# First LayerNorm's inverse deviations by way of DRAM instead of the TensorE, with seven interleaved blocks

## The chip, the core and the metric

The kernel runs on one core of a Trainium2 chip. The metric is the device time in microseconds (us) of the whole launch; lower is better. Before the change three runs took 2405.96 us in the median (2402.36 to 2407.58). Engine names in the profile: PE is the TensorE's matmul side and PEld its weight loads, DVE is the VectorE, ACT the ScalarE, POOL the GpSimd, SP the SyncE, which only issues DMAs here.

## What is computed

Layer 0 adds to `x` (32 images, 56 x 56 places, 128 channels, f32) a convolution of its binarised group norm. Layer 1 reads the result as 32 x 3136 tokens of 128 channels and adds causal attention in windows of 64 tokens, and then an expert layer fed by 8 tokens for each of 64 experts. Cut to what matters:

```python
x = x + _L0_conv_ref(_gn(x), L0_conv_gamma, L0_conv_beta, L0_conv_W)
t = _to_tokens(x)
t = t + _L1_attn_ref(_ln_t(t), L1_attn_w_qkv, L1_attn_w_proj, L1_attn_b_proj)
t = t + _L1_ffn_ref(_ln_t(t), L1_ffn_gate_w, L1_ffn_gate_b, L1_ffn_weight1, L1_ffn_weight2)

def _ln_t(v, eps=1e-5):
    m = jnp.mean(v, axis=-1, keepdims=True)
    s = jnp.var(v, axis=-1, keepdims=True)
    return (v - m) / jnp.sqrt(s + eps)
```

The change concerns the first `_ln_t`, the one ahead of the attention. The mean's part is folded into centred weights ahead of the loop, so the kernel only multiplies each token by its inverse deviation.

## The kernel before

**Preparation** (lines 164 to 330). All of `x` is read once, in 16 loads of 3136 KB, for the statistics of the group norm; small products turn them into the thresholds `thr_a` and `thr_b`. SP's queue holds these 16 loads, then the loads of the main loop.

**Main loop** (lines 933 to 1022). The 32 images form 16 pairs; a block is 8 rows of a pair, so a pair has 7 blocks and there are 112. A block holds 2 x 448 tokens, as 7 units of 128 (64 tokens of each image). One turn of the loop works on several blocks at once: while block n is in its attention, later blocks are in earlier stages. With `n` the turn:

- `load` (line 463): block n+6 comes in, 2 DMAs of 224 KB on SP, into `xb` (two buffers).
- `bits` (475): block n+5 is turned to channels first (7 transposes `xT_ps`), copied by ACT (`xT`, `bn`) and binarised by DVE (`hbits`).
- `conv` and `residual` (502, 516): 9 products of block n+3, and `yT = xT + conv` on DVE. `conv` is split, 4 taps after `scores` and 5 after `norm1`.
- `norm1` (531): block n+2 is turned back (`yt`), DVE takes `bn_stats` of its 7 units, and POOL raises the variances to -0.5 (`inverse_std`, line 426). The result `rstd1` has a token on each partition: 128 x 7.
- `normalise` (534): block n+1. The next products want channels on partitions, so every channel's row needs all 896 inverse deviations. Seven transposes of a broadcast column write them to the PSUM tile `rr`, and DVE multiplies `rr` by `yT` into `n1T`.
- `queries_or_keys`, `values` (543, 561): products of `n1T`, each copied out by ACT.
- `scores` (598): block n; 4 mask products and 56 x 2 small products into two PSUM tiles, and two ACT exponentials `pT`.
- `attend` (631): the products `av` of `pT` and the values, then DVE's `rs` and `ao`; `turn_out`, `project`, `norm2` (658 to 695): `aoT`, `pj`, DVE's `tT`, the turn `tt`, ACT's copy `tok`, second LayerNorm statistics, and stores of `tok` on POOL's queue (to the output) and on SP's (to `toks`).
- `gate_logits` (697): block n-1, the products `lg`.

The order on PE, DVE, ACT, SP and POOL is the order of the program text (`manual_schedule`), so an instruction that waits holds up all behind it on its engine. PSUM tiles made by `bank2` rotate through three buffers. In one turn PE's order is `sc`, 4 taps `cv`, `rr`, `lg`, `av`, `xT_ps`, `qT_ps`, `aoT_ps`, `kT_ps`, `v_ps`, `pj`, `yt`, 5 taps `cv`, `tt`.

**A pair's end.** Over the 13 turns after a pair's last block its steps run in between (lines 898 to 924): `spread` sends the second LayerNorm's deviations to DRAM and back as rows (`devs`, `drow`), then come the largest 8 gate values, the gather of their tokens (`gather`, POOL), shares, and stores. In turns 1 to 8 the loop also fills the DRAM tensor `share` with zeros, 1024 KB a turn.

**Expert stage** (lines 1029 to 1193). After the loop the pooled tokens go through the experts and the results are added at their places in the output.

Of the kernel before, what the change touches and what calls it, by code (L numbers as in the profile page):

```python
# [17 lines left out]
P = 128  # L18
HEADS = 4
HD = 32  # L20
# [10 lines left out]
def kernel(  # L31
# [39 lines left out]


    ident = const.tile([P, P], F32, name="ident")
    make_identity(nc, ident)
# [7 lines left out]

    head1 = const.tile([P, HEADS, HD], F32, name="head1")
    nc.vector.memset(head1, 1.0)
# [10 lines left out]

    g4 = const.tile([P, P // 4, 4], F32, name="g4")
    nc.vector.memset(g4, 0.25)
# [10 lines left out]

    tri = const.tile([P, 2, P], F32, name="tri")
    nc.vector.memset(tri, 0.0)  # L110
# [53 lines left out]
    with tc.tile_pool(name="prep", bufs=1) as prep, tc.tile_pool(  # L164
# [118 lines left out]
        def scaled(b0, b1):  # L283
# [3 lines left out]
            nc.vector.tensor_mul(vr[:, bs], vr[:, bs], rg[:, bs])  # L287


        TP = 2 * S // P  # L290
        x2 = x.rearrange("b h w c -> (b h w) c").rearrange("(n p j) c -> n p j c", p=P, j=TP)
        for pr in range(NPAIR):
            xb = xs.tile([P, TP, C], F32, name="xb")
            nc.sync.dma_start(out=xb, in_=x2[pr])
            st = xs.tile([P, 2, NB, 6], F32, name="st")
            for g in range(NB):
                pt = xps.tile([P, 2, 512], F32, name="pt").rearrange("p a (s c) -> p (a s) c", c=P)
                for j in range(NU):
                    nc.tensor.transpose(pt[:, j, :], xb[:, g * NU + j, :], ident)
                for i in range(2):  # L300
                    nc.vector.bn_stats(st[:, i, g, :], pt[:, :NU, i * WIN : (i + 1) * WIN])  # L301
            for i in range(2):
                nc.vector.bn_aggr(
                    mv[:, 2 * pr + i, :], st[:, i].rearrange("p g s -> p (g s)")
                )
            if pr == NPAIR - 4:
                group_norm(0, B - 8)
            if pr == NPAIR - 2:
                scaled(0, B - 8)
        group_norm(B - 8, B)  # L310
        scaled(B - 8, B)
# [18 lines left out]
        nc.vector.tensor_scalar(thr_b, thr_b, off, None, ALU.add)  # L330


    slots = [dram.tile([P, K], F32, name=f"slots{i}") for i in range(NPAIR)]
    putrow = [dram.tile([P, K], U32, name=f"putrow{i}") for i in range(NPAIR)]
    grows = dram.tile([NQ, P, NPAIR, P], F32, name="grows")

    share = dram.tile([NQ, P, NPAIR, 2, ES], F32, name="share")
    toks = [dram.tile([2, S, P], F32, name=f"toks{i}") for i in range(NPAIR)]
    eout = dram.tile([E, B, P], F32, name="eout")
    obias_d = dram.tile([P, NG, P], F32, name="obias_d")  # L340
    devs = [dram.tile([2, NB * NU, WIN], F32, name=f"devs{i}") for i in range(NPAIR)]

# [24 lines left out]
    def main_loop(fast):  # L367
        with ExitStack() as main:
# [17 lines left out]
            )  # L386
            yTp = loop.enter_context(tc.tile_pool(name="yTp", bufs=4))
            w1 = loop.enter_context(tc.tile_pool(name="w1", bufs=1))
# [8 lines left out]
            def units(t):  # L397

                return t.rearrange("p a (s c) -> p (a s) c", c=P)[:, :NU, :]
# [9 lines left out]
            nc.gpsimd.memset(vblk, 1.0)  # L409
            zero = first.tile([P, 4 * P], F32, name="zero")  # L410
            nc.gpsimd.memset(zero, 0.0)

# [45 lines left out]
            class Block:  # L458
# [16 lines left out]
                def bits(self):  # L475

                    pr, r = self.pr, self.r
                    xT_ps = turn(self.xb, "xT_ps")
                    self.xT = xTp.tile([P, 2, BT], F32, name="xT")
                    nc.scalar.activation(  # L480
                        self.xT.rearrange("c i (p j) -> c i p j", j=NU),
                        units(xT_ps).rearrange("c j (i p) -> c i p j", p=WIN),
                        AF.Identity, bias=conv_nb,
                    )
                    bn = w1.tile([P, 2, RB, W], F32, name="bn")
                    for i in range(2):
                        b = 2 * pr + i
                        nc.scalar.activation(  # L488
                            bn[:, i].rearrange("c h (g j) -> c h g j", j=NU),
                            units(xT_ps)[:, :, i * WIN : (i + 1) * WIN].rearrange(  # L490
                                "c j (h g) -> c h g j", h=RB
                            ),
                            AF.Identity, bias=thr_b[:, b : b + 1], scale=thr_a[:, b : b + 1],
                        )
                    bit = w1.tile([P, RB, W], FP16, name="bit")
                    nc.vector.tensor_scalar(bit, bn[:, 0], 0.0, 1.0 / FINE, ALU.is_ge, ALU.mult)
                    nc.vector.scalar_tensor_tensor(
                        hbits[pr % 2][:, 1 + r * RB : 1 + (r + 1) * RB, 1 : 1 + W],
                        bn[:, 1], 0.0, bit, ALU.is_ge, ALU.subtract,
                    )  # L500
# [30 lines left out]
                def norm1(self):  # L531
                    self.rstd1 = unit_stats(units(turn(self.yT, "yt")), "ln1")

                def normalise(self):
                    rr = bank2("rr")
                    for u in range(NU):
                        nc.tensor.transpose(  # L537
                            units(rr)[:, u, :], self.rstd1[:, u : u + 1].to_broadcast([P, P]), ident
                        )
                    self.n1T = w1.tile([P, NU, P], F32, name="n1T")  # L540
                    nc.vector.tensor_mul(self.n1T, units(rr), self.yT)

# [164 lines left out]
            class Pair:  # L707
# [9 lines left out]
                def spread(self, r0, r1):  # L717
# [3 lines left out]
                    nc.tensor.transpose(dT_ps, self.devs[:, r0 * NU : r1 * NU], ident)  # L721
                    dT = wp.tile([m, P], F32, name=f"dT{m}")
                    nc.scalar.copy(dT, dT_ps)
# [143 lines left out]
                def shares(self, ks):  # L867

                    if ks[0] == 0:
                        self.sh = gatep.tile([P, E, K], F32, name="sh")  # L870
                    src = self.srow
# [60 lines left out]

            for n in range(-6, N + 1):
                this, nxt, conv, prev = at(n), at(n + 1), at(n + 3), at(n - 1)

                steps = [(n - pr * NB - NB + 1, pair) for pr, pair in pairs.items()]
                steps = [(j, pair) for j, pair in steps if 1 <= j <= 13]
                ends = dict(steps)
                if at(n + 6):
                    at(n + 6).load()  # L940
                if 0 < n <= NQ:
                    nc.sync.dma_start(
                        out=share[n - 1].rearrange("p n i s -> p (n i s)").rearrange(
                            "p (a s) -> p a s", s=4 * P
                        ),
                        in_=zero.unsqueeze(1).to_broadcast([P, NPAIR * 2 * ES // (4 * P), 4 * P]),
                    )
                if n == N // 8:
# [35 lines left out]
                if this:  # L984
                    this.attend()
                if at(n + 5):
                    at(n + 5).bits()
                if this and this.r == NB - 1 and n < N - 1:
# [23 lines left out]
                if this:  # L1012
                    this.project()
                if at(n + 2):
                    at(n + 2).norm1()
                if conv:
# [224 lines left out]
```

## Time and profile before

| what | value |
|---|---|
| median of three runs | 2405.96 us (2402.36 to 2407.58) |
| the profiled execution's own time | 2399.98 us |
| its span in the profile | 2398.2 us |
| PE / DVE / ACT / POOL busy in the span | 90% / 74% / 48% / 34% |
| mean granted TensorE clock | 0.959 |
| DMA share in the loop, by slices | 0.3 to 0.6 |
| preparation, up to the first `xT_ps` of the loop | 0 to 166 us |
| first to last `av` (112 blocks) | 201.5 to 2123 us |
| expert stage | from about 2145 us to the end |

In a group's row of the profile stand the line, engine, operation, output<-inputs, shapes and count, then the busy time and the mean of one instruction in ns, and the idle time before them with what ended it. In a row of the timeline the first number is the start and the second the duration, in us. A turn of the loop lasts 17.1 to 17.4 us for nearly all blocks, counted from one `av` to the next.

### The profile page before, as it was taken

How to read it: one execution, taken by the hardware profiler on the slowest of the kernel's cores; microseconds unless marked ns; L12 is line 12 of the kernel's file. 1: busy time of each engine (PE TensorE's matmuls, PEld its weight loads, DVE VectorE, ACT ScalarE, POOL GpSimd, SP SyncE). 2: the span in 40 equal slices, each digit the busy share in tenths (PEclk: the TensorE clock that was granted, in tenths of full speed). 3: DMA queues.
4: the chain of work that ended last, by engine and by line, in shares of the span. 5: the costliest groups of instructions: out<-in, count | busy, mean ns of one | idle time of the engine just before them, and what ended most of it. 6: DMA issues, size and time to landing. Idle time of an engine off the chain costs nothing.

```text
span 2398.2 us, 82838 instructions
## 1 busy us (share of the span) xinstructions
PE 2164.7 (90%) x35865; PEld 1524.2 (64%) x35865; DVE 1777.1 (74%) x4974; ACT 1159.6 (48%) x1683; POOL 814.3 (34%) x772
## 2 busy tenths in 40 slices
PE   6769999999999999999999999999999999954452
PEld 5656676667676666667676666666666767632332
DVE  7975567788888888888887878787878787775221
ACT  0015555555555556565655565656555555432210
POOL 1012223242424242424242333333333333334556
PEclk9989999999999999999999999999999999977776
DMA  9943464544444445454545363636363535647961
GB/s 367 393 153 84 138 166 101 119 112 107 109 111 105 115 102 118 99 120 97 122 98 122 82 137 80 139 80 139 79 137 81 135 84 127 189 124 259 356 231 58
DMA packets 238300, 334.31 MB, mean 139 GB/s; under 512 B 50598, under 2 KB 175206, under 8 KB 231654
## 3 DMA queue, kind: packets, MB, share of 16 engines
q1 hardware_dynamic: 207878, 254.56, 38.1%
q0 software_dynamic: 27648, 72.38, 13.0%
q8 instruction: 285, 4.67, 0.8%
q10 hardware_dynamic: 2400, 1.97, 0.3%
q14 instruction: 89, 0.73, 0.1%
HBM read 195.14 MB, written 134.74 MB: 138 GB/s over the span
## 4 chain that ended last, share of the span: by engine, by line
PE 77%; ACT 7%; DVE 6%; DMA 5%; issue 3%; POOL 2%; SPq 0%; POOLq 0%; ACTq 0%; DVEq 0%
PE cv L509 8%; PE av L639 8%; PE kT_ps L550 8%; PE pj L673 8%; PE v_ps L566 7%; PE sc L590 6%; PE xT_ps L440 4%; PE lg L701 4%; PE yt L440 4%; ACT bn L488 4%; PE rr L537 4%; PE tt L440 3%; ACT xT L480 3%; DVE st L301 3%; PE sc L579 2%
## 5 line engine op out<-in xcount | busy, mean ns | idle before, releaser
L426 POOL TENSOR_TENSOR ln_rstd<-ln_var,nhalf 128x7 f32<-128x7 f32 x112 | 167.6, 1496 | 924.9 <-DVE ln_var L423 609.4
L480 ACT ACTIVATE xT<-xT_ps,conv_nb 128x896 f32<-128x896 f32 x112 | 112.8, 1007 | 406.4 <-PE xT_ps L440 250.2
L426 POOL TENSOR_TENSOR devs<-ln_var,nhalf 128x7 f32<-128x7 f32 x112 | 165.7, 1479 | 266.4 <-DVE ln_var L423 266.4
L605 ACT ACTIVATE pT<-sc 128x896 f32<-128x896 f32 x224 | 193.2, 915 | 119.9 <-PE sc L590 118.9
L639 PEld LDWEIGHTS av<-vblk,pT 64*64 64x64 f32 x12544 | 195.7, 135 | 86.3 <-ACT pT L605 77.1
L509 PE MATMUL cv<-hbits,wconv 128*128 128x448 f16 x1008 | 233.0, 358 | 11.9 <-DVE s L524 5.6
L566 PEld LDWEIGHTS v_ps<-wqkvT,n1T 128*128 128x128 f32 x1568 | 192.7, 192 | 41.6 <-issue 41.6
L639 PE MATMUL av<-vblk,pT 64*64 64x33 f32 x12544 | 209.7, 221 | 6.2 <-issue 5.2
L679 DVE SCALAR_TENSOR_TENSOR tT<-pj,bproj_c,yT 128x448 f32<-128x448 f32 x224 | 142.7, 678 | 85.0 <-PE pj L673 85.0
L550 PE MATMUL kT_ps<-n1T,wqkvT 128*128 128x448 f32 x448 | 197.6, 563 | 5.5 <-PE aoT_ps L662 1.0
L673 PE MATMUL pj<-aoT,wprojT 64*128 64x448 f32 x896 | 200.2, 566 | 1.1 <-ACT aoT L665 1.1
L522 ACT ACTIVATE s<-cv,conv_mid 128x448 int32<-128x448 f32 x112 | 70.8, 632 | 257.1 <-PE cv L509 257.1
L566 PE MATMUL v_ps<-wqkvT,n1T 128*128 128x128 f32 x1568 | 193.1, 275 | 0.0
L550 PE MATMUL qT_ps<-n1T,wqkvT 128*128 128x448 f32 x448 | 188.1, 542 | 0.1
L692 POOL DMA_DIRECT2D out_dram<-tok x224 | 169.1, 756 | 0.1
L590 PE MATMUL sc<-qT,kT 32*64 32x64 f32 x12544 | 166.9, 233 | 0.0
L433 DVE BATCH_NORM_STATS2 ln_st<-yt 128x6 f32<-128x128 f32 x784 | 164.9, 280 | 2.5 <-PE yt L440 2.5
L590 PEld LDWEIGHTS sc<-qT,kT 32*64 32x64 f32 x12544 | 151.4, 130 | 22.7 <-issue 22.7
L433 DVE BATCH_NORM_STATS2 ln_st<-tok 128x6 f32<-128x128 f32 x784 | 161.8, 278 | 5.0 <-ACT tok L687 4.9
L1129 POOL DMA_INDIRECT out_dram<-f_rows,rowidx x128 | 123.8, 967 | 81.6 <-DVE f_rows L1125 44.7
L488 ACT ACTIVATE bn<-xT_ps,thr_b,thr_a 128x448 f32<-128x448 f32 x224 | 149.3, 720 | 2.6 <-DVE thr_b L330 2.4
L526 DVE SCALAR_TENSOR_TENSOR yT<-s,conv_s,xT 128x448 f32<-128x448 f32 x224 | 143.5, 682 | 4.0
(187 smaller groups left out, 4082.9 us busy)
## 6 DMA issues: line engine op xcount, KB each, us to landing
xb<-in_x_dram SPq DMA_DIRECT2D x16, 3136.0 KB
xb<-in_x_dram SPq DMA_DIRECT2D x224, 224.0 KB
toks<-tok SPq DMA_DIRECT2D x224, 224.0 KB
out_dram<-tok POOLq DMA_DIRECT2D x224, 224.0 KB, 3.5
u<-in_L_ffn_weight_dram SPq DMA_DIRECT2D x16, 2048.0 KB
drow<-devs SPq DMA_DIRECT2D x30, 672.0 KB
share<-zero SPq DMA_DIRECT2D x8, 1024.0 KB
grows<-rows SPq DMA_DIRECT2D x32, 256.0 KB
```

Of the source, the lines that this page charges most:

```text
L426: nc.gpsimd.tensor_tensor(rstd, var, nhalf[:, :n], ALU.pow)
L433: nc.vector.bn_stats(st[:, u, :], src[:, u, :])
L440: nc.tensor.transpose(units(t)[:, u, :], src[:, u, :], ident)
L480: nc.scalar.activation(self.xT.rearrange("c i (p j) -> c i p j", j=NU), units(xT_ps).rearrange("c j (i p) -> c i p j", p=WIN), AF.Identity ...
L488: nc.scalar.activation(bn[:, i].rearrange("c h (g j) -> c h g j", j=NU), units(xT_ps)[:, :, i * WIN : (i + 1) * WIN].rearrange("c j (h g) ...
L509: nc.tensor.matmul(self.cv[:, :BT], lhsT=wconv[:, t, :], rhs=hb[:, r * RB + kh : r * RB + kh + RB, kw : kw + W], start=(t == 0), stop=(t = ...
L550: nc.tensor.matmul(pp[:, a, :BT], lhsT=wqkvT[:, s, :], rhs=flat[:, a * BT : (a + 1) * BT], start=True, stop=True,)
L566: nc.tensor.matmul(units(vp)[:, u, :], lhsT=self.n1T[:, u, :], rhs=wqkvT[:, 2, :], start=True, stop=True,)
L590: nc.tensor.matmul(tiles[h // 2][part, h % 2, u * WIN : (u + 1) * WIN], lhsT=left[hp, u, part], rhs=right[hp, u, part], start=False, stop= ...
L605: nc.scalar.activation(pT, rows2(sc), AF.Exp, scale=HD ** -0.5)
L639: nc.tensor.matmul(av[h % 2 * WIN : (h % 2 + 1) * WIN, i, m * VW : (m + 1) * VW], lhsT=self.pT[h // 2][rows, h % 2, u, :], rhs=self.vb[row ...
L673: nc.tensor.matmul(pj[:, i, :BT], lhsT=wprojT[rows, g, :], rhs=self.aoT[rows, :, g, :], start=(g == 0), stop=(g == 1),)
```

## The change

`normalise` has no products any more. `norm1` writes `rstd1` (128 x 7) from SP to a DRAM tensor of its own block, `rdev[n]`, and a second SP DMA reads it back as one row of 896 numbers, repeated on all 128 partitions, into the SBUF tile `rr` (two buffers). The row is in the order token, unit; DVE's product reads it with the unit as the outer dimension, so along a unit it takes every seventh number.

Every stage ahead of `normalise` is a block earlier: `load` n+7, `bits` n+6, `conv` n+4, `norm1` n+3, and the loop begins at turn -7. `yT` has five buffers instead of four. `normalise` stays at n+1.

Room is made for it. Three constants are freed after the preparation (`head1`, `g4`, `tri`, in the pool `once`). `bn` and `bit` live in the pool `first`. `dT` is one tile instead of two. A pair's shares `sh` have one buffer in `wp` instead of two in `gatep`, and the last pair's take the place of a `logits` tile. The zeros of `share` are no longer written in turns 1 to 8: eight SP DMAs of 1024 KB write them in the preparation, from a tile of 128 x 2048, behind the 16 loads of `x` and ahead of the loop's first loads.

```diff
@@ in the preparation
+        zero = prep.tile([P, NPAIR * 2 * ES], F32, name="zero")
+        nc.gpsimd.memset(zero, 0.0)
...
             if pr == NPAIR - 2:
                 scaled(0, B - 8)
+        for q in range(NQ):
+            nc.sync.dma_start(out=share[q].rearrange("p n i s -> p (n i s)"), in_=zero)
         group_norm(B - 8, B)
...
+    rdev = [dram.tile([P, NU], F32, name=f"rdev{i}") for i in range(NPAIR * NB)]
...
-            yTp = loop.enter_context(tc.tile_pool(name="yTp", bufs=4))
+            yTp = loop.enter_context(tc.tile_pool(name="yTp", bufs=5))
...
                 def norm1(self):
-                    self.rstd1 = unit_stats(units(turn(self.yT, "yt")), "ln1")
+
+                    rstd1 = unit_stats(units(turn(self.yT, "yt")), "ln1")
+                    nc.sync.dma_start(out=rdev[self.n], in_=rstd1)
+                    self.rr = w2.tile([P, P, NU], F32, name="rr")
+                    nc.sync.dma_start(
+                        out=self.rr.rearrange("c p u -> c (p u)"),
+                        in_=rdev[self.n].rearrange("(o p) u -> o (p u)", o=1).to_broadcast([P, P * NU]),
+                    )
 
                 def normalise(self):
-                    rr = bank2("rr")
-                    for u in range(NU):
-                        nc.tensor.transpose(
-                            units(rr)[:, u, :], self.rstd1[:, u : u + 1].to_broadcast([P, P]), ident
-                        )
                     self.n1T = w1.tile([P, NU, P], F32, name="n1T")
-                    nc.vector.tensor_mul(self.n1T, units(rr), self.yT)
+                    nc.vector.tensor_mul(self.n1T, self.yT, self.rr.rearrange("c p u -> c u p"))
...
                     if ks[0] == 0:
-                        self.sh = gatep.tile([P, E, K], F32, name="sh")
+                        if self.pr < NPAIR - 1:
+                            self.sh = wp.tile([P, E, K], F32, name="sh")
+                        else:
+                            sh = gatep.tile([P, S], F32, name="logits")
+                            self.sh = sh[:, : E * K].rearrange("p (e k) -> p e k", k=K)
...
-            for n in range(-6, N + 1):
-                this, nxt, conv, prev = at(n), at(n + 1), at(n + 3), at(n - 1)
+            for n in range(-7, N + 1):
+                this, nxt, conv, prev = at(n), at(n + 1), at(n + 4), at(n - 1)
...
-                if at(n + 6):
-                    at(n + 6).load()
-                if 0 < n <= NQ:
-                    nc.sync.dma_start(
-                        out=share[n - 1].rearrange("p n i s -> p (n i s)").rearrange(
-                            "p (a s) -> p a s", s=4 * P
-                        ),
-                        in_=zero.unsqueeze(1).to_broadcast([P, NPAIR * 2 * ES // (4 * P), 4 * P]),
-                    )
+                if at(n + 7):
+                    at(n + 7).load()
...
-                if at(n + 5):
-                    at(n + 5).bits()
+                if at(n + 6):
+                    at(n + 6).bits()
...
-                if at(n + 2):
-                    at(n + 2).norm1()
+                if at(n + 3):
+                    at(n + 3).norm1()
```

## The prediction, made before the changed kernel ran

> **What bounds the kernel now.** I read the slices first, then the chain of waits, then one block in the timeline.
>
> ```profile
> PE 2164.7 (90%) x35865; PEld 1524.2 (64%) x35865; DVE 1777.1 (74%) x4974; ACT 1159.6 (48%) x1683; POOL 814.3 (34%) x772
> PE   6769999999999999999999999999999999954452
> PEclk9989999999999999999999999999999999977776
> PE cv L509 8%; PE av L639 8%; PE kT_ps L550 8%; PE pj L673 8%; PE v_ps L566 7%; PE sc L590 6%; PE xT_ps L440 4%; PE lg L701 4%; PE yt L440 4%; ACT bn L488 4%; PE rr L537 4%; PE tt L440 3%; ACT xT L480 3%; DVE st L301 3%; PE sc L579 2%
> ```
>
> In the 31 slices of the loop PE is always busy, at full clock; the chain runs through nearly every PE group in turn, `rr` with 4%. So a product taken from PE's list shortens a turn, unless the next instruction on PE then waits. The timeline of PE, ACT and DVE from `scores` to `attend` of one block tells:
>
> ```profile
> 1011.42 1.46 PE L590 MATMUL sc<-qT,kT 32*64 32x64 f32 x112
> 1012.82 0.94 PE L509 MATMUL cv<-hbits,wconv 128*128 128x448 f16 x4
> 1013.59 0.93 PE L537 MATMUL rr<-ident,ln_rstd 128*128 128x128 f32 x7
> 1014.45 0.97 PE L701 MATMUL lg<-tT,gateT 128*64 128x448 f32 x4
> 1015.35 1.84 PE L639 MATMUL av<-vblk,pT 64*64 64x33 f32 x112
> ...
> 1012.95 1.73 ACT L605 ACTIVATE pT<-sc 128x896 f32<-128x896 f32 x2 [1.01 <-PE sc L590]
> ...
> 1015.41 1.08 DVE L541 TENSOR_TENSOR n1T<-rr,yT 128x896 f32<-128x896 f32 x1
> 1017.25 0.33 DVE L647 RECIPROCAL rs<-av 128x28 f32<-128x28 f32 x1 [0.76 <-PE av L639]
> ```
>
> `rr` starts 0.86 us ahead of `lg`, `lg` 0.90 ahead of `av`. But `av` needs `pT`, which ACT begins only when `sc` is done and ends at 1012.95 + 1.73 = 1014.68. Now `av` comes 0.67 later than that, so nobody waits.
>
> **What a turn gains.** Without `rr` PE would be ready for `av` at 1015.35 - 0.86 = 1014.49, but `pT` ends at 1014.68. A ready `av` starts at once: in block 0, which has no `lg`, `pT` ended at 201.51 and `av` began at 201.53. So `av` moves to about 1014.70, and 0.65 us is gained, not 0.86; 0.2 us becomes a new wait of PE on ACT. Over the blocks `av` starts 0.60 to 0.71 after `pT`, mostly 0.65 to 0.68: I take **0.63 us a turn**.
>
> **DVE is next.** `n1T` ends at 1016.49, the last `av` at 1017.19. With `av` 0.65 earlier DVE's spare time of 0.70 shrinks to 0.05: `rs` still is not held up. Behind it stands `ao` (ends 1018.77) and PE's weight load of `aoT` at 1019.07, another 0.30. So if the new `n1T` is x us longer, PE feels only what x has above 0.05 + 0.30, say 0.36 with rounding: the gain of a turn is 0.63 - max(0, x - 0.36), and nothing is left at x = 0.99. After that DVE waits for ACT's `bn`, which absorbs it.
>
> **The price of the new `n1T`** is the main unknown: both inputs are now in SBUF (PSUM before), one read with 28 bytes from number to number. DVE's groups:
>
> ```profile
> L541 DVE TENSOR_TENSOR n1T<-rr,yT 128x896 f32<-128x896 f32 x112 | 121.2, 1082 | 5.4 <-PE rr L537 5.4
> L879 DVE TENSOR_TENSOR sh<-sh,sh 128x512 f32<-128x512 f32 x112 | 77.6, 693 | 3.8
> L526 DVE SCALAR_TENSOR_TENSOR yT<-s,conv_s,xT 128x448 f32<-128x448 f32 x112 | 76.7, 685 | 4.0
> L679 DVE SCALAR_TENSOR_TENSOR tT<-pj,bproj_c,yT 128x448 f32<-128x448 f32 x224 | 142.7, 678 | 85.0 <-PE pj L673 85.0
> L751 DVE TENSOR_TENSOR logits<-logits,drow 128x3136 f32<-128x3136 f32 x15 | 51.3, 3417 | 0.0
> L886 DVE COPY pooled<-pl 128x128 f32<-128x128 f32 x16 | 6.0, 374 | 40.7 <-PE pl L883 40.7
> L423 DVE TENSOR_TENSOR g_var<-g_var,g_dif 128x8 f32<-128x8 f32 x16 | 2.7, 167 | 0.5
> L849 DVE TENSOR_TENSOR g_mean<-g_st 128x8 f32<-128x8 f32 x16 | 2.6, 166 | 0.0
> ```
>
> From SBUF alone, 512 numbers took 693 ns and 3136 took 3417, 1.04 ns each; 896 would take 693 + 384 x 1.04 = 1092 ns. That is today's 1082. For the stride: line 849 reads both inputs 24 bytes apart, and its 8 numbers take 166 ns against 167 for the packed line 423, so no cost (lower end, x = 0.01). Line 886 reads and writes with long strides (its input in PSUM): 374 ns for 128 numbers, where the copy of line 1069 (512 in 689 ns) would need 689 - 384 x 1.04 = 290; 0.66 ns a number, x = 0.59 for 896 (upper end from a row). I take x = 0.01, since line 849 is the same operation with the same kind of operands and nearly the same stride, though short.
>
> The Trainium skill, "SBUF — State Buffer", Door 1, speaks against the change: accesses that each fall on a new 16-byte line pay a penalty, and 28 bytes always do. It gives DVE no figure; line 849 shows none. The same page, Who interferes with whom, says that a DVE instruction with two SBUF inputs and a GpSimd instruction that reads SBUF exclude each other for a whole instruction. Row against rule: `yT` (line 526, two SBUF inputs) runs beside POOL's power of `ln_rstd` in the block above (from 1012.24, and 1011.86 to 1013.37) and takes 676 to 686 ns in all 224 cases, like line 679, which reads one input from PSUM. By the rule one of `n1T` and POOL's power would stand still: the sum stays at the forecast if that is POOL, and is that of the third rival below if it is `n1T`; by the rows neither stands.
>
> **The detour.** POOL's power ends at 1013.37; two SP issues follow (0.3 to 0.6 us each, as lines 725 and 731 have). The second waits for the first one's landing:
>
> ```profile
> SPq L692 <- ACT tok L687: 1040.4, 110, 22.6
> SPq L731 <- DMA devs<-dT: 44.0, 31, 4.7
> ```
>
> Line 725's store, the like of `rdev`, was issued at 1037.73 and its reader at 1041.08, 3.4 us; 4.7 is the longest wait of SP there. The read of `rr` is 128 x 3584 bytes, as much as a block's two `xb` loads, 448 KB; I give it 3 us. That is about 8 us from the power to `rr`. `normalise` is two turns on: its `n1T` of the same block starts 2.0 us after the power now, one turn more makes 18. So 10 us are spare; each further us would cost PE one. Behind the waiting SP stand the stores of `toks` (first read by the gather five turns on) and the next `xb` load (used a turn later); SP waits 1040 us / 112 = 9.3 us a turn for `tok` today and gives up some 5 of them. The DMA engines get 28 GB/s more; at 0.48 share for some 110 GB/s that is a share of 0.12 more. No cost; with that cover gone, up to the 5 us a turn by which SP is longer.
>
> **Moved edits.** Zeros: 8.4 MB at 334 GB/s (the rate in 220 to 224 us, where one such store ran) to 393 (the first slices) are 21 to 25 us. The last `x` load is in by about 140, and from 145 to 165 the engines move 0 to 3 GB/s. The zeros then end at 161 to 165, the first `xb` loads 2.5 later. The first `xT_ps` ran at 165.65, but `bn` waited for `thr_b` until 170.92: 0, at worst +3; I take +0.5. The memset (128 x 2048 took 1.79 in line 1157) lies in POOL's idle 114 us. `sh` with one buffer is rewritten two turns after its store is issued, which lands in 2.7 to 7.5 us; `dT`, `bn`, `bit`, five `yT`: 0.
>
> The extra turn at the front: the first three blocks' `cv` began at 173.31, 179.97 and 187.17, so one more such turn is 7.2; turn -1 no longer has `rr` (188.21 to 190.0), -1.6. **+5.6** (2 to 8). At the end work runs out a turn earlier. From the `av` of block 106 to that of 111 it now takes 17.11 + 16.29 + 17.48 + 17.34 + 14.93 = 83.2, with PE waiting for POOL ahead of `rr` (0.45, 0.52) and 1.2 after it. Without `rr`, `xT_ps` (0.82) and the last taps a turn sooner I get 15.7 + 15.7 + 15.4 + 15.0 + 14.9 = 76.7; I take **-5** (-3 to -6.5).
>
> **Sum.** 105 turns x -0.63 = -66.2; -5; +5.6; +0.5: -65. On the profiled execution (2399.98, span 2398.2) that makes 2335. It lay 6 us below the median of the runs, 2405.96, which becomes **2341 us**.
>
> **Rivals.**
> - *Moderate stride cost*, x = 0.4 to 0.8 (line 886's 0.59): a turn gains 0.59 to 0.19, 2345 to 2386; at 0.59, 0.40 a turn, 2365. For it: line 886; against: line 849.
> - *Half rate*, a second 1.04 ns for each strided number: x = 0.93, a turn gains 0.06: 2400, 2392 to 2412. DVE takes PE's place as the bound.
> - *Slower: `n1T` waits for POOL.* The power of `devs` starts at 1015.57, 0.16 after `n1T`, in every block and lasts 1.48. If `n1T` stood until 1017.05, it would end at 1018.13, x = 1.64; a turn loses 0.65: 2406 + 68 = 2474. It decides from x = 0.99 on. Against it: line 526's even 676 to 686 ns.
> - *Slower: `rr` late.* If SP's chain took 20 instead of 8 us, each turn would lose 2 us less 0.63: over 2500. Against it: the 10 us of spare.
> - *The change saves `rr` whole*, 0.86 a turn: 2317. It would need `pT` earlier, which nothing brings; its share is inside my forecast's.
>
> **Chances.** Forecast 0.57; moderate 0.13; half rate 0.14 (0.05 faster, 0.07 the same, 0.02 slower); POOL 0.11; late `rr` 0.05. Faster by over 0.2% (4.8 us, about the spread of the three runs): 0.57 + 0.13 + 0.05 = 0.75; the same 0.07; slower 0.18. The likeliest case alone spans 2328 to 2354. The range must take in the moderate and the half rate to leave under 0.2 out: 2324 to 2411.
>
> **What would show it.** `n1T` near 1.09 us; `av` starting 0.03 after the end of `pT` in nearly every block, with PE idle about 0.2 there; turns of 16.5 us; SP's wait for `rdev`'s landing at 3 us without PE ever waiting behind it; first `av` 5 us later. I am wrong if `n1T` is over 1.45 us, if PE's weight load of `aoT` waits for `ao`, or if DVE waits for `rr`.

## The result, and the profile after

The changed kernel takes 2434.57 us in the median of four runs (2425.73 to 2438.09), the kernel before 2406.47 beside it (2402.36 to 2407.58): a ratio of 1.0114, with a 95% interval of 1.0084 to 1.0145. The change made it slower by about 28 us, where 65 us of gain were forecast. The profiled execution took 2436.53 us, its span 2434.7; before it was 2399.98 and 2398.2. So 36.5 us of span have to be found.

The page of the changed kernel, engine totals and two rows of slices:

```profile
PE 2125.0 (87%) x35081; PEld 1463.3 (60%) x35081; DVE 1856.2 (76%) x4974; ACT 1161.7 (48%) x1683; POOL 982.6 (40%) x772
PE   6768999899999999999999999999999998854452
PEclk9989999999999999999999999999999999976676
```

PE has 40 us less work than before (2164.7) and a span that is 36 longer. The group of `rr` alone had been busy for longer than that:

```profile
L537 PE MATMUL rr<-ident,ln_rstd 128*128 128x128 f32 x784 | 105.6, 275 | 1.1 <-POOL ln_rstd L426 1.0
```

Other products have grown in turn (`qT_ps` 208.0 us from 188.1, `av` 227.1 from 209.7). Slices of 60 us hide where it stands still. Turns show it: the time from one `av` to the next, sorted by the block's place in its pair (0 to 6), in us, worked out from the trace's `av` starts.

| stretch | before | after |
|---|---|---|
| up to the first `av` | 201.5 | 210.6 |
| 74 turns from a block 1 to 5, to block 104, mean | 17.19 | 16.57 |
| the turn from block 15 (loads of `hbias`) | 21.5 | 30.2 |
| 15 turns from a block 6, mean | 17.48 | 17.59 |
| 15 turns from a block 0 (the one after a pair's end), mean | 17.48 | **21.04** |
| five turns from block 106 to 111 | 83.1 | 89.0 |
| from the last `av` to the end | 278.7 | 282.2 |

74 turns gain 0.62 us each, 46 us in all, almost the forecast's 0.63. The 15 turns after a pair's end lose 3.56 each, 53 us: more than the whole gain. The rest is 9 us at the front, 9 in one turn, and 11 in the last five turns, in the stretch after the last `av` and in the turns from block 6.

An ordinary turn, from the timeline of the changed kernel (start, duration, engine, line):

```profile
997.69 1.73 ACT L615 ACTIVATE pT<-sc 128x896 f32<-128x896 f32 x2 [1.01 <-PE sc L600]
998.43 0.97 PE L711 MATMUL lg<-tT,gateT 128*64 128x448 f32 x4
999.33 1.86 PE L649 MATMUL av<-vblk,pT 64*64 64x33 f32 x112
1000.17 1.81 DVE L551 TENSOR_TENSOR n1T<-yT,rr 128x896 f32<-128x896 f32 x1
1000.33 3.00 POOL L434 TENSOR_TENSOR devs<-ln_var,nhalf 128x7 f32<-128x7 f32 x1 [2.26 <-DVE ln_var L431]
1001.89 0.32 DVE L657 RECIPROCAL rs<-av 128x28 f32<-128x28 f32 x1
1003.70 0.93 PE L672 MATMUL aoT_ps<-ident,ao 128*128 128x128 f32 x7
1004.46 1.75 PE L560 MATMUL kT_ps<-n1T,wqkvT 128*128 128x448 f32 x4
```

`av` follows `lg` at once. `n1T` now takes 1.81 us and holds `rs` until 0.7 us after the last `av`; POOL's power, which starts 0.16 us after `n1T`, lasts 3.00 us in place of 1.48. Yet `kT_ps` comes 5.13 us after `av`, against 5.08 before. The waits of PE's weight load ahead of it, before and after (us in total, times, longest), tell why:

```profile
PEld kT_ps L550 <- ACT bn L488: 27.8, 105, 0.3
```

```profile
PEld kT_ps L560 <- ACT bn L496: 8.6, 32, 0.3
```

`aoT_ps`, which needs `rs`, comes 0.25 us later (4.34 after `av`, from 4.09, in the median of ordinary turns), and most of that is used up where PE had waited for ACT before.

A turn after a pair's end, first as a chain of waits (start, us, what held):

```profile
1063.66 1.42 PE sc L600 x75
1065.08 0.87 PE cv L517 x4
1065.95 0.90 PE lg L711 x4
1066.85 0.83 PE av L649 x43
1067.68 2.97 issue
1070.66 2.14 PE av L649 x69
1072.80 1.69 PE xT_ps L448 x7
```

then as busy times by stretch (PE, PEld, DVE, ACT, POOL, then the granted clock, the DMA engines' share and GB/s):

```profile
1062.00:1067.50 5.50, 5.50 (x177) 3.60 (x175) 5.33 (x24) 3.80 (x5) 1.50 (x1) 1.00 1.05 237
1067.50:1070.66 3.16, 0.19 (x12) 0.08 (x4) 1.85 (x2) 0.00 (x0) 2.91 (x1) 0.94 0.07 6
1070.66:1077.30 6.64, 6.64 (x81) 4.93 (x81) 2.39 (x5) 2.36 (x4) 1.50 (x3) 0.51 0.81 218
1077.30:1090.00 12.70, 12.70 (x210) 8.40 (x212) 8.50 (x30) 7.21 (x9) 1.50 (x1) 1.00 0.20 53
```

PE stops after 43 of the 112 products of one and the same `av`: no data is late, since the products ahead and behind read the same tiles. The profile calls it "issue". Ahead of the stop all 16 DMA engines are busy (share 1.05). After it PE works 6.6 us at a clock of 0.51, in which `xT_ps` and `qT_ps` take nearly twice as long. What the DMA engines did from 1061 to 1067.5, and from there to 1070.7, by queue (packets, MB, share):

```profile
q1 hardware_dynamic: 144, 1.38, 92.1%
```

```profile
q1 hardware_dynamic: 160, 0.00, 4.3%
q8 instruction: 1, 0.02, 2.6%
```

The first is `drow`: two broadcast loads of 672 KB (line 741), a burst of 5.5 us. As soon as it ends, one packet of 16 KB goes through the queue called instruction, and 2.5 us later PE goes on. Such a packet comes 279 times in the run, once for every 251 of PE's instructions (products and weight loads); in the kernel before it came 285 times, once for every 252. That is why I read this queue as the one that brings PE's instructions. One `av` has 224 of them. In the 13 stops of over 1 us within `av` in this trace PE went on 2.4 to 2.9 us after the start of such a packet, every time.

The burst stood there before as well, but its last packet started 1.6 to 4.0 us ahead of the `av` of block 0 in 14 of the 15 turns (7.1 in the other). Why it is later is in the waits of SP and PE (us in total, times, longest):

```profile
SPq L542 <- POOL ln_rstd L434: 806.6, 109, 12.9
SPq L544 <- DMA rdev<-ln_rstd: 230.5, 112, 6.4
SPq L741 <- DMA devs<-dT: 84.8, 31, 9.3
```

```profile
PE av L649 <- issue: 46.6, 18, 6.8
PE dT_ps L731 <- POOL devs L434: 17.0, 17, 1.3
```

The first of PE's was in the kernel before:

```profile
PE av L639 <- issue: 5.2, 7, 2.8
```

SP now waits for POOL's result, which comes 15.4 us after `av` (median), where `tok`, for which it waited before, is there at 13.9. Then it waits 2.1 us a turn for the landing of `rdev`. Everything behind it moves: ahead of a pair's end, `toks` of the block before is issued 18.3 us after its `av` (before: 13.9), in the turn from block 6 `devs` at 7.7 (5.3), and `drow`, which also waits longer for the landing of `devs`, at 11.2 (7.1). The burst then lies at 11 to 20 us after `av`, across the next `av`.

### The profile page after: what moved, and what is told of

It is laid out like the page before. It is cut to its first block, busy times and chain, and to the rows that moved or that the text cites. A ratio compares the mean times of both kernels' runs of the same rounds, so it can differ in the third digit from the quotient of the medians.

```text
span 2434.7 us, 81650 instructions
## 1 busy us (share of the span) xinstructions
PE 2125.0 (87%) x35081; PEld 1463.3 (60%) x35081; DVE 1856.2 (76%) x4974; ACT 1161.7 (48%) x1683; POOL 982.6 (40%) x772
## 4 chain that ended last, share of the span: by engine, by line
PE 67%; DVE 12%; issue 8%; DMA 5%; POOL 4%; ACT 2%; SPq 1%; ACTq 0%; POOLq 0%; DVEq 0%
PE av L649 7%; PE cv L517 6%; PE qT_ps L560 6%; PE pj L683 6%; PE kT_ps L560 6%; PE v_ps L576 6%; PE sc L600 6%; PE xT_ps L448 4%; PE yt L448 3%; PE lg L711 3%; DVE st L308 3%; PE tt L448 3%; PE aoT_ps L672 3%; POOL devs L434 2%; PE pt L306 2%
## 5 line engine op out<-in xcount | busy, mean ns | idle before, releaser
L434 POOL TENSOR_TENSOR devs<-ln_var,nhalf 128x7 f32<-128x7 f32 x112 | 330.4, 2950 | 247.1 <-DVE ln_var L431 235.4
L649 PEld LDWEIGHTS av<-vblk,pT 64*64 64x64 f32 x12544 | 209.8, 139 | 134.2 <-ACT pT L615 83.7
L649 PE MATMUL av<-vblk,pT 64*64 64x33 f32 x12544 | 227.1, 225 | 50.1 <-issue 46.6
L560 PE MATMUL qT_ps<-n1T,wqkvT 128*128 128x448 f32 x448 | 208.0, 590 | 2.9 <-DVE n1T L551 2.7
L551 DVE TENSOR_TENSOR n1T<-yT,rr 128x896 f32<-128x896 f32 x112 | 201.9, 1803 | 0.0
L600 PE MATMUL sc<-qT,kT 32*64 32x64 f32 x12544 | 172.2, 234 | 3.6 <-issue 3.6
```

Of the source, the lines that this page charges most:

```text
L434: nc.gpsimd.tensor_tensor(rstd, var, nhalf[:, :n], ALU.pow)
L551: nc.vector.tensor_mul(self.n1T, self.yT, self.rr.rearrange("c p u -> c u p"))
L560: nc.tensor.matmul(pp[:, a, :BT], lhsT=wqkvT[:, s, :], rhs=flat[:, a * BT : (a + 1) * BT], start=True, stop=True,)
L600: nc.tensor.matmul(tiles[h // 2][part, h % 2, u * WIN : (u + 1) * WIN], lhsT=left[hp, u, part], rhs=right[hp, u, part], start=False, stop= ...
L649: nc.tensor.matmul(av[h % 2 * WIN : (h % 2 + 1) * WIN, i, m * VW : (m + 1) * VW], lhsT=self.pT[h // 2][rows, h % 2, u, :], rhs=self.vb[row ...
```

## Experiments

The kernel before ran beside each group; its median there was 2401 to 2405 us, and each ratio is against those runs.

**1. SP's order.** `rdev` is written a turn later, when POOL's result has long been there, and `rr` is read just ahead of `attend`:

```diff
+                def send(self):
+                    nc.sync.dma_start(out=rdev[self.n], in_=self.rstd1)
+                def fetch(self):
+                    self.rr = w2.tile([P, P, NU], F32, name="rr")
...
                     at(n + 7).load()
+                if at(n + 2):
+                    at(n + 2).send()
...
+                if at(n + 2):
+                    at(n + 2).fetch()
                 if this:
                     this.attend()
```

> The changed kernel with another order on SP: the write of rdev and the read of rr are issued one turn's start later, behind the stores of toks and the next xb load, so that these two and all behind them no longer stand behind the wait for rdev's landing. Theory 'late rows' (SP's wait pushes the 1.3 MB burst of drow to 11 to 14 us behind av, where it blocks the fetch of PE's instructions just when scores and attend use them up): the burst begins 8 to 10 us behind av again, the turn from a pair's first av falls from 20.8 to 17 to 17.5 us, and the total falls by 50 to 70 us to 2365 to 2385. Rival 'traffic' (the 448 KB that rr adds to each turn are what starves PE): nothing changes, 2425 to 2440. Rival 'lock' (POOL's stretched powers hold PE up): nothing changes.

Measured: 2414.31 us, ratio 1.0046 (1.0028 to 1.0065). The front came down by 0.4 only, the turns after a pair's end to 19.66. The burst lay at 10.8 to 18.7 us, not back at 8 to 14: `devs` was issued at 5.7, nearly as before, but `drow` at 10.3, since `devs` landed late beside the read of `rr`.

**2 and 3. Traffic alone, chain alone.** In the first, `rr` comes from one constant row in DRAM, with no write and no wait; in the second `rdev` is written and read back to one partition, and `n1T` multiplies by a constant tile with the same stride. Both leave out the first LayerNorm.

```diff
-                    nc.sync.dma_start(out=rdev[self.n], in_=rstd1)
...
-                        in_=rdev[self.n].rearrange("(o p) u -> o (p u)", o=1).to_broadcast([P, P * NU]),
+                        in_=rdev.rearrange("(o p) u -> o (p u)", o=1).to_broadcast([P, P * NU]),
```

```diff
-                        out=self.rr.rearrange("c p u -> c (p u)"),
-                        in_=rdev[self.n].rearrange("(o p) u -> o (p u)", o=1).to_broadcast([P, P * NU]),
+                        out=self.rr[0:1].rearrange("c p u -> c (p u)"),
+                        in_=rdev[self.n].rearrange("(o p) u -> o (p u)", o=1),
...
-                    nc.vector.tensor_mul(self.n1T, self.yT, self.rr.rearrange("c p u -> c u p"))
+                    nc.vector.tensor_mul(self.n1T, self.yT, rfix.rearrange("c p u -> c u p"))
```

> The changed kernel without the write of rdev: rr is read each turn from one row of constants in DRAM (0.03, so the first LayerNorm is left out), with the same 448 KB, but SP has nothing to wait for. 'Late rows': the stalls in av at a pair's first block go, 2355 to 2385. 'Traffic': they stay, 2420 to 2440. 'Lock': n1T and POOL's powers as before, stalls stay.

> The changed kernel with the write of rdev and SP's wait for its landing, but read back into one partition only (3.5 KB in place of 448 KB); n1T reads a constant tile of 0.03 with the same stride, so the first LayerNorm is left out. 'Late rows': SP is as late as in the changed kernel, the stalls stay for the larger part, 2400 to 2435. 'Traffic': they go, 2355 to 2385.

Measured: 2409.15 (ratio 1.0014, 0.9995 to 1.0033) and 2407.72 (1.0008, 0.9989 to 1.0027). Of the 3.56 us lost in a turn after a pair's end they give back 61 and 50% (18.86 and 19.26 us, from 21.04), neither all of it. The time of run 2 lies in neither of its two ranges, that of run 3 in the one for 'late rows'. So it is not one of the two: both push the burst, `drow` being issued at 8.7 and 9.9 us. In run 2 the read of `rr` is issued at 10.0, right behind it, and the instruction packet comes 1.8 to 2.7 us after the start of the burst's last packet (0.2 to 0.9 in the changed kernel).

**4. Packed numbers.** `n1T` reads `rr` without the stride, and so each channel gets the deviations in the wrong order:

```diff
-                    nc.vector.tensor_mul(self.n1T, self.yT, self.rr.rearrange("c p u -> c u p"))
+                    nc.vector.tensor_mul(self.n1T, self.yT, self.rr.rearrange("c p u -> c (p u)").rearrange("c (u p) -> c u p", u=NU))
```

> The changed kernel with n1T reading rr in its packed order (the inverse deviations then meet the wrong tokens). If the stride costs the 0.72 us of n1T: 1.09 us, POOL's power of devs falls from 2.95 to about 2.2, the wait of dT_ps for it in a pair's last block (1.0 us) shrinks to 0.3, total 5 to 20 us less than the changed kernel. If the lock with POOL costs it: n1T stays at 1.80. Both theories of the stalls expect the stalls at a pair's first block to stay.

Measured: 2434.94, ratio 1.0139 (1.0116 to 1.0162), no gain. Its groups of instructions (busy us, mean ns of one, idle before):

```profile
L434 POOL TENSOR_TENSOR devs<-ln_var,nhalf 128x7 f32<-128x7 f32 x112 | 250.7, 2239 | 249.8 <-DVE ln_var L431 238.2 <-PE av L649 11.6
L551 DVE TENSOR_TENSOR n1T<-yT,rr 128x896 f32<-128x896 f32 x112 | 121.3, 1083 | 0.0
```

against the changed kernel's:

```profile
L434 POOL TENSOR_TENSOR devs<-ln_var,nhalf 128x7 f32<-128x7 f32 x112 | 330.4, 2950 | 247.1 <-DVE ln_var L431 235.4 <-PE av L649 11.6
L551 DVE TENSOR_TENSOR n1T<-yT,rr 128x896 f32<-128x896 f32 x112 | 201.9, 1803 | 0.0
```

and the power in the kernel before:

```profile
L426 POOL TENSOR_TENSOR devs<-ln_var,nhalf 128x7 f32<-128x7 f32 x112 | 165.7, 1479 | 266.4 <-DVE ln_var L423 266.4
```

The stride costs 720 ns, and POOL's power follows `n1T` (711 ns less where `n1T` is 720 shorter). In both runs it ends 1.34 to 1.35 us after the end of `n1T` (medians), little less than the 1.48 that it takes alone: POOL stands still while `n1T` lasts. The turns from block 6 fell from 17.59 to 16.88, since `dT_ps` waits for that power (17.0 us in all in the changed kernel, 5.6 here). But the burst lay no earlier, the turns after it took 21.7 us, and the gain was gone. The loss sits in the burst, not on DVE.

**5. The burst later, in the kernel before.** `drow` is issued behind that turn's `toks`:

```diff
+                        if self.pr < NPAIR - 1:
+                            return
+                    self.rows_of(r0, r1)
+                def rows_of(self, r0, r1):
...
                     this.norm2(pairs[this.pr])
+                    if this.r == NB - 1 and n < N - 1:
+                        pairs[this.pr].rows_of(0, NB - 1)
```

> The kernel before, with one thing changed: SP issues drow's two loads of six rows of deviations after that turn's toks stores instead of right behind the store of devs. Nothing is added. Theory 'late burst' (the kernel lost in the turns in which drow's 1.3 MB leave the DMA engines no room for the instruction fetch that PE needs within av): the burst now ends past the next av, PE stands in that av as in the changed kernel, the 16 turns after a pair's last block grow from 17.5 to 21-23 us, the time by 50 to 75 us, to some 2460. Rival 'traffic' (it takes the 448 KB more a turn): burst later, PE not held, no change within 10 us.

Measured: 2406.57, ratio 1.0017 (0.9998 to 1.0036). My theory in this form was wrong: it asked for stops. The burst lay at 0 to 8 us after the start of the `av` of block 0, over the whole of it, and PE did not stop there: the instruction packet had come 2.5 us (median) ahead of that `av`, before the burst. So a burst beside `av` is harmless; what counts is where the packet falls. In 12 of the traces (all but the two that have other stops, h and i below), for the 180 turns after a pair's end, with the first packet from 5 us ahead of `av` on:

| start of the instruction packet, from the start of `av` | turns | mean turn, us |
|---|---|---|
| over 0.5 us ahead | 98 | 17.7 |
| 0.5 ahead to 0.2 behind | 24 | 19.1 |
| 0.2 to 1 behind | 26 | 20.2 |
| 1 to 2 behind | 21 | 21.0 |
| 2 to 3.5 behind | 11 | 22.5 |

**6. The burst twice, in the kernel before.** The test of that:

```diff
-                    for i in range(2):
+                    for i in range(2) if r0 or self.pr == NPAIR - 1 else (0, 1, 0, 1):
                         nc.sync.dma_start(
```

> The kernel before, with drow's two loads of six rows issued twice over (same rows, same place), 15 times in all; nothing else. The burst then lasts from 8 to about 20 us after av instead of 8 to 14, so it lies over the 3 us ahead of the next av, where the instruction fetch was seen to start. Theory 'fetch behind the burst': PE stops 2 to 5 us within that av, then runs some microseconds at a clock of 0.5; 15 turns of 20 to 23 instead of 17.4 us, 40 to 80 us more, 2445 to 2485. Rival (late_rows showed that a burst over the start of av alone costs nothing): no stop, the time within 8 us of 2405.

Measured: 2445.71, ratio 1.0188 (1.0156 to 1.0220). None of the added parts of the change is in this kernel, and its turns after a pair's end take 20.61 us. One of them in its chain of waits and its stretches (same columns as above):

```profile
824.17 3.02 issue
827.18 1.51 PE av L639 x49
828.70 1.69 PE xT_ps L440 x7
830.38 0.21 PE dT_ps L721
830.60 2.80 PE qT_ps L550 x4
```

```profile
814.00:828.40 14.40, 11.38 (x272) 7.96 (x272) 9.47 (x33) 4.70 (x6) 4.44 (x4) 0.93 0.94 205
828.40:833.00 4.60, 4.60 (x24) 3.09 (x21) 2.19 (x5) 2.36 (x4) 0.00 (x0) 0.50 0.74 265
```

The same stop within `av` and the same half clock behind it. In all its 12 stops PE went on 2.3 to 3.0 us after the packet's start.

**7. The burst earlier, in the changed kernel.** `drow` is issued at the head of the next turn, behind `xb` (with `rows_of` as in 5):

```diff
                     at(n + 7).load()
+                if this and this.r == 0 and this.pr:
+                    pairs[this.pr - 1].rows_of(0, NB - 1)
```

> The changed kernel, with drow's two loads of six rows issued at the head of the next turn, behind its xb load; the store of devs has landed by then. Theory 'late burst': the burst lies between two av, PE's stops within av go (except in the turn of the hbias loads), the turns after a pair's last block come down from 20.8 to 17-18 us: 16 x 3 to 4 us less, some 2375 to 2390. Rival 'traffic' or 'late rows': those turns keep their 20 us, the time stays above 2420.

Measured: 2392.55, ratio 0.9953 (0.9935 to 0.9971), 42 us below the changed kernel (39 by the two ratios) and the first to beat the kernel before. The burst lies at 7 to 15 us between two `av`, the packets 0.6 to 2.2 ahead of `av`, the turns take 17.89. PE's stops within `av` are gone from these turns; what is left there is POOL:

```profile
PE dT_ps L731 <- POOL devs L434: 33.5, 30, 1.3
```

**8. The depth alone.** The changed kernel with the seven products of the kernel before, no `rdev`, no `rr` from DRAM:

```diff
-                    nc.sync.dma_start(out=rdev[self.n], in_=rstd1)
...
+                    rr = bank2("rr")
+                    for u in range(NU):
+                        nc.tensor.transpose(
+                            units(rr)[:, u, :], self.rstd1[:, u : u + 1].to_broadcast([P, P]), ident
+                        )
...
```

> The changed kernel with everything that was moved (zeros at the start, one more block in advance, five yT, narrower pools) but with the seven PE products of the kernel before; no rdev, no rr read. Theory: turns as in the kernel before (17.1 us), burst 8 to 10 us after av, no stops in av; first av 9 us later (210), the end a few us shorter: 2408 to 2418. Rival: the depth itself delays SP, then the turns after a pair's last block are 19 us or more and the time is above 2425.

Measured: 2410.6, ratio 1.0026 (1.0013 to 1.0038), as expected: turns after a pair's end of 17.40, first `av` at 210.2. So the 9 us at the front come with the depth and the moved work, not with `rr`; and since the first `xT_ps` ran at 165.41 us in the changed kernel and at 165.65 before, the zeros ahead of it cost nothing there.

**9 to 12. Towards a faster kernel.** Four versions, all with the early burst. In h PE turns `rstd1` to 7 x 128 late in the turn and DRAM gets packed rows; in i SP scatters `rstd1` in pieces of 4 bytes instead; in i, k and l the loads of `hbias` and `obias_d` are cut into eighths; l is k with h's product right behind `av`, and the burst behind `rr`.

```diff
+                def send(self):
+                    rT_ps = pcv.tile([P, 512], F32, name="rT_ps", tag="lg")[:NU, :P]
+                    nc.tensor.transpose(rT_ps, self.rstd1, ident)
+                    rT = w2.tile([NU, P], F32, name="rT")
+                    nc.scalar.copy(rT, rT_ps)
+                    nc.sync.dma_start(out=rdev[self.n], in_=rT)
...
-                    nc.vector.tensor_mul(self.n1T, self.yT, self.rr.rearrange("c p u -> c u p"))
+                    nc.vector.tensor_mul(self.n1T, self.yT, self.rr)
```

```diff
-                    nc.sync.dma_start(out=rdev[self.n], in_=rstd1)
+                    nc.sync.dma_start(out=rdev[self.n].rearrange("u p -> p u"), in_=rstd1)
```

```diff
+                if n in (16, 17, 23, 24, 30, 31, 37, 38):
+                    k = (16, 17, 23, 24, 30, 31, 37, 38).index(n)
+                    es = slice(k * E // 8, (k + 1) * E // 8)
                     nc.sync.dma_start(
-                        out=hbias,
+                        out=hbias[:, es],
```

```diff
                     this.attend()
+                if at(n + 2):
+                    at(n + 2).send()
+                if this and this.r == 0 and this.pr:
+                    pairs[this.pr - 1].rows_of(0, NB - 1)
```

> As f_early_rows, and n1T reads packed numbers: PE turns rstd1 (128x7) to 7x128 in one product a turn later, ACT copies it, SP writes rows of 512 bytes and reads them back to all partitions; rr has one buffer. Computes the whole of the reference. Expected: n1T 1.08 us as in the packed run, no wait of PE for POOL ahead of dT_ps, turns of 16.3 to 16.6 us with about 17.5 after a pair's last block, 2345 to 2370. If the late rows or the traffic matter by themselves it ends above 2400.

> As f_early_rows, but SP writes ln_rstd scattered, 4 bytes at a time, so that the row in DRAM lies unit by unit and n1T reads packed numbers without a product or a copy; and the loads of hbias and obias_d are cut into eighths over eight calm turns. Computes the whole of the reference. If the stride and the burst are the two losses: n1T 1.08 us, POOL's power of devs near 2.2 us, no wait ahead of dT_ps, turns 16.4, after a pair's last block 17.0, no turn of 30 us; 2350 to 2370. If 896 pieces of 4 bytes land too late: SP's wait for rdev's landing grows from 1.7 to over 6 us a turn and the gain is lost again, above 2400.

> As f_early_rows, and the loads of hbias and obias_d, which stood at the head of one turn (34 us in f_early_rows, 21 in the kernel before), are cut into eighths over eight calm turns. Computes the whole of the reference; the strided read stays. If that turn was long because its many small pieces stood ahead of rr and the instruction fetch: the turn comes down to about 17 us, the others stay, 2392 - 15 = some 2377. If it only moves: the eight turns gain 2 us each and the time stays at 2392.

> As k_split, with packed numbers for n1T: right behind av PE turns rstd1 (128x7) in one product, ACT copies 7x128, SP writes it and reads it back to all partitions, drow's burst follows behind. In h_best the same product came later in the turn, its read of rr lay beside the instruction fetch of the next av, and pl waited for the shared PSUM tile. Computes the whole of the reference. Expected: n1T 1.08, SP's wait for POOL gone, no wait of PE for POOL ahead of dT_ps, turns of 16.5 with 17 after a pair's last block, no stops within av; 2345 to 2360. If the product and the copy cost as much as the stride: 2375 or more.

Measured: h 2435.96 (1.0141, 1.0111 to 1.0171), i 3109.0 (1.2962, 1.2904 to 1.3019), k 2374.97 (0.9881, 0.9854 to 0.9908), l **2363.27** (0.9838, 0.9810 to 0.9866). h and i fell far from what I expected. h, its waits:

```profile
DVE n1T L557 <- DMA rr<-rdev: 35.3, 11, 13.1
PE av L655 <- issue: 28.0, 20, 6.9
PE pl L909 <- ACT rT L547: 15.5, 14, 1.4
```

`rr` was issued only 11.4 us after `av`, came too late for DVE in 11 turns, and its own transfer lay beside the instruction packet of the next `av`; and `pl` waited in 14 turns for the PSUM tile that `rT` shared. l, the same work at the other end of the turn, has no stop of over 1 us within `av`, no such wait of `pl`, and DVE waits for `rr` in two turns only (10.5 us). i, the waits of PE and of SP:

```profile
PE av L649 <- issue: 355.3, 144, 7.8
```

```profile
SPq L544 <- DMA rdev<-ln_rstd: 1021.8, 102, 13.1
```

896 pieces of 4 bytes a turn land in some 10 us, and PE stops 144 times, within or right ahead of 73 of the 112 `av`. Here the packets do not tell when it goes on (0.3 to 12.7 us after the start of the last one, in the 88 stops of over 1 us), so what holds PE in i is not shown. l, its groups and waits of SP:

```profile
L434 POOL TENSOR_TENSOR devs<-ln_var,nhalf 128x7 f32<-128x7 f32 x112 | 250.1, 2233 | 257.6 <-DVE ln_var L431 257.6
L557 DVE TENSOR_TENSOR n1T<-yT,rr 128x896 f32<-128x896 f32 x112 | 121.3, 1083 | 10.5 <-DMA rr<-rdev 10.5
```

```profile
SPq L708 <- ACT tok L703: 596.3, 88, 16.7
SPq L550 <- DMA rdev<-rT: 208.1, 112, 13.4
```

`n1T` is back at 1083 ns, SP is mostly waiting for `tok` again as in the kernel before, and the turns are 16.67 (blocks 1 to 5), 16.96 (block 6) and 17.43 (block 0) us. l computes the whole of the reference and beats both kernels.

## Why the prediction was wrong, step by step

- **What a turn gains: right in size, not in its bound.** The 74 ordinary turns gained 0.62 us on average, the calmest 0.71. The calmest exceed 0.63 because `av` does not wait for the end of `pT`: it began at 999.33, `pT` ended at 997.69 + 1.73 = 999.42. I took the rule "starts once `pT` has ended" from block 0 alone. `pT` is two tiles, and `av`'s first products need the first one. That the average meets my 0.63 is in part luck: with the measured `n1T` (x = 0.72) my own rule for DVE would have left 0.63 - 0.36 = 0.27.
- **DVE's slack: too small.** I let a turn pay for every microsecond of `n1T` above 0.36. `n1T` grew by 0.72 and an ordinary turn paid next to nothing (`kT_ps` 0.05 us later), because PE had waited up to 0.3 us for ACT's `bn` ahead of `kT_ps`, a wait that I had left out.
- **The price of `n1T`: mis-sized.** I took x = 0.01 from line 849, with eight numbers; it was 0.72, above my upper bound of 0.59 (run 4: without the stride 1083 ns). In an instruction of eight numbers 0.80 ns a number would be 6 ns, no more than the rows of that size differ among themselves (164 to 172 ns): the upper row, with 128, was far nearer. `n1T` was over the 1.45 us that I had named as a sign of being wrong, but the loss was not there. The Trainium skill, "Vector Engine (DVE) Microarchitecture Reference", 5.2, which I did not weigh, has 1.73 ns a column where one source hops by 4 KiB at every element, against 1.05; worked out from it, an estimate, 896 x 0.68 = 0.61. The runs show (1803 - 1083) / 896 = 0.80 ns a number.
- **POOL beside `n1T`: "by the rows neither stands" was wrong.** POOL stood (1479 to 2950 ns, and to 2239 with the packed `n1T`). In my row POOL had started first; here `n1T` starts 0.16 us ahead of it, and unlike in the kernel before both its inputs are in SBUF. The rule of the Trainium skill, "SBUF — State Buffer", Who interferes with whom, which I had set against the row, held in this order. In the other order it did not show: in the changed kernel `yT` runs 194 times beside a power of POOL that had started first, and takes 678 to 686 ns as ever. And a POOL that stands did not leave the sum alone: `dT_ps` in the turns from block 6 waits for it up to 1.3 us, so that 15 turns stayed at 17.59 instead of falling to 16.88, some 11 us. The rival in which `n1T` stands did not occur.
- **The detour: "No cost" is the step that failed.** I had seen that SP would be later, up to 5 us a turn, and looked for those who wait for `rr`, `toks` and `xb`. SP was 4.4 us late for `toks`, `drow` was issued 4.0 us later, and `drow`'s data is waited for only once (DVE, 4.2 us). But I did not name `devs` and `drow` among what stands behind SP's wait, and did not ask what the burst would meet at its new place. It met the instruction packet of the next `av`: 15 turns x (21.04 - 17.48) = 53 us, where the sum had -9.5. My other measure, a mean DMA share of 0.12 more, could not show it: the burst takes all 16 engines for 5.5 us. The turn with the loads of `hbias` adds 8.7, also with a longer stop within `av` (6.8 us, before 2.8); with the loads cut into eighths it fell from 33.9 (run 7) to 16.4 us (run 11), while two of the eight turns that took the pieces came to 18.8 and 19.8.
- **Moved edits: a little low.** +9.0 at the front where I had 5.6 + 0.5. The extra turn is there; beyond it the first `xT_ps` behind it waited 1.15 us for `xb`, and `qT_ps` took 3.19 us there, against 1.81. The end, forecast at -5, came out at +5.9 and +3.5. The depth alone showed part of it (84.9 in the five last turns against 83.1, and 282.4 from the last `av` to the end, a stretch that lies between 277.6 and 286.2 over all runs); the rest was not taken apart.

The misses add up: 15 turns after a pair's end 63 us, 15 from block 6 11, block 15 9, the end 11 + 3.5, the front 3, together 101; forecast -65 and measured +36.5 differ by 101.5.

Of the rivals, none named the mechanism. "`rr` late" came nearest, with SP's chain as its cause, but no `rr` was late in the changed kernel: DVE never waited for it.

## What to carry to other kernels

When a step on a DMA queue gets longer, list every transfer behind it on that queue, and ask for each large one where in time it lands, not only who waits for its data. A stop called "issue" in the middle of a run of like instructions pointed to the instruction queue here: compare the start of its packets with the bursts ahead of them, and move a burst so that the packet for the next dense stretch comes in time (some 40 us here, for one moved call). A row with eight numbers gives no price per number.

## What the runs showed of the hardware

- PE's instructions come through a DMA queue of their own (by the count of its packets, above), in packets of 16 KB, which wait behind a burst that holds all 16 DMA engines. In the seven kernels whose burst is compact (5.8 us in the median from the start of its first packet to that of its last; both kernels and runs 1 to 4 and 8) three instruction packets began within the 105 bursts, all in the last 0.5 us, where their mean rate in the loop would make some 83; in the changed kernel the next began 0.2 to 0.9 us after the start of the burst's last packet, in all 15 cases. Where other transfers mix into the burst (some 7 us, runs 7, 11 and 12), packets get in, fewer than by their rate. PE went on 2.3 to 3.0 us after the packet's start in all 39 stops of over 1 us within `av` in the changed kernel and runs 6 and 4 (13, 12 and 14). Run i, where every turn has 896 small stores, does not follow this.
- A stop can cost more than itself, because PE then runs at half the clock (0.51 and 0.50 in the stretches above). Of the 39 stops, 33 were followed by 3.4 to 13.7 us of it: all 20 from 2.97 us on, and 13 of the 19 shorter ones, the shortest of 1.9 us. The Trainium skill, "TensorE: Matmul & The Clock Gate", Part 1, has half the clock after at least one idle window of some 3.4 us; here shorter stops were enough.
- Two inputs in SBUF, one of them with 28 bytes from number to number: 1803 ns for 896 numbers, against 1083 packed. Packed from SBUF or from PSUM made no difference (1083, 1082).
- 896 stores of 4 bytes a turn, 3.5 KB in all, in place of 128 of 28 bytes: 3109 us against 2375 (run i against k, which differ in that store and in the order of the row, and so in how `n1T` reads it).
